# Attention values by seven block products, and a block's transfers issued from SP's queue

## The chip, the cores and the metric

The kernel runs on one core of one Trainium2 chip. The metric is the device time of one execution in microseconds (us). The median of three runs of the kernel before is 2158.83 us (2158.8 to 2162.86).

## The reference

The input `x` has 2048 rows of 256 numbers, in f32. It is normalized row by row, and two results are added to it:

```python
xn = layernorm(x)                                  # [2048, 256]
q, k, v = heads(xn @ Wqkv.T)                       # 16 heads, head size 128
w = softmax(q @ k.T / sqrt(128))                   # per head, [2048, 2048]
attn = concat(w @ v) @ Wout.T                      # Wout: [256, 2048]
ffn = bitlinear(sigmoid(bitlinear(xn, w1)) * bitlinear(xn, w2), w3)   # ternary weights, hidden 704
out = x + attn + ffn
```

## The kernel before

**Stages.** A lead-in of some 120 us normalizes `x`, keeps it transposed in SBUF (`xnT`, 128 partitions x 2 halves of the 256 features x 2048 rows), makes queries, keys and values of the first heads, and does the whole feed-forward part; its result goes to four DRAM tiles `yd0` to `yd3`, one for each 512 rows. Everything after that is attention.

**Blocks, quarters, groups.** A block is 512 query rows of one head: 16 heads x 4, 64 blocks. A block has four quarters of 128 rows. Two heads, that is 8 blocks, are a group, and 8 groups follow one another. One turn of the main loop is called a step here and named (block in its group, quarter): (1,3) is the last quarter of a group's second block. The order on every engine is the order in which the program's text issues, and every engine and queue works strictly in it.

**One step.** In step (b, t) TensorE does, in this order: the scores of a quarter six steps ahead (`scores`: 16 matmuls of 512 columns); a first side product; the weighted sum of this step's own quarter of the block (`weighted`, line 724: 32 matmuls of 256 columns, 16 in t = 3); a second side product, in most steps. VectorE does the reads that the step before left behind (`added`, lines 750 and 754, and the read of the second side product), two row maxima of the scores (line 579), their scale (582), the read of the first side product, in t = 2 the inverses of the softmax sums (624 to 627), and two transposes (line 657) of the quarter two steps back. ScalarE does the exponentials (589).

**The exchange.** The weights must be turned round. VectorE transposes only inside squares of 32 x 32, so each quarter's exponentials `p` are first moved between partitions into tiles `part`, by 12 DMAs of 64 KB. `exchanged` issues ten of them from SP's queue and two from ScalarE's (line 611). `part` has two buffers; an exchange thus needs that the transposes of two quarters back have been done.

**Products with fewer multiplications.** The weighted sum is done by a scheme of seven block products in place of eight; GpSimd makes the block differences for it (`differences`, line 677, in `R`; `v_combined`, line 699, in `st`). Queries and keys of the next head are made the same way (`fast_product`), four matmul instructions of 512 columns a product, from sums of `xnT` (`x_sums`, held in `ts`) and of the weights. So are the output projections of the group before (`o_product`, read by `o_read`, line 824). The values of the next group are made directly (`v_product`: 16 matmul instructions of 256 columns, two row tiles of both heads).

**Side products by place.** In quarters 2 and 3 of every block: queries and keys. In quarters 0 and 1 of blocks 0 to 3 of a group: output products of the group before. In quarters 0 and 1 of blocks 4 to 7: values of the next group. All side products use one PSUM buffer (`ps_m`, tag m), and the weighted sum another (`ps_av`); each is written anew only when its readers are done.

**What is moved about.** Attention results of a block go from `oU` to DRAM (`put_away`: `od`), and come back into three slots `o3` for the output products (`o_fetched`). The running sums of the output sit in `yd0` to `yd3`, and two at a time in SBUF (`osums`): `y_moved` loads or stores one of 512 KB. `inverses` stores the inverses of the softmax sums (`rd`) and `spread` loads them back spread over partitions (`oT`). `load_weights` loads 256 KB. All of these are issued from GpSimd's queue; their places are in the loop's body and in `between(n, t)`, which runs at the end of a step, after `exchanged`:

```python
if (a, t) == (0, 0):
    y_moved(b + 1, False)
...
elif (a, t) == (1, 0):
    o_fetched(g, b + 1, 1, 0)
...
elif (a, t) == (1, 3) and more:
    y_moved(b + 2, False)
```

Here `a` is the block's parity and `b` the even block, in blocks 0 to 3 of a group.

Of the kernel before, what the change touches and what calls it, by code (L numbers as in the profile page):

```python
# [20 lines left out]
def layernorm_attention_bitffn_kernel(  # L21
# [132 lines left out]

    def x_sums(c: int):
        t = apool.tile([P, 4, QB], F32, tag=f"t{c}", name=f"t{c}", bufs=1)
        x00, x10 = (xnT[:, d, bass.ts(c, QB)] for d in range(KC))
        x01, x11 = (xnT[:, d, bass.ts(c + 1, QB)] for d in range(KC))
        for i, (a, b) in enumerate(((x01, x00), (x11, t[:, 0]), (x11, x01), (x10, t[:, 1]))):
            nc.gpsimd.tensor_tensor(t[:, i], a, b, ALU.subtract)  # L160
        ts[c] = t

    def fast_product(h: int, b: int, i: int, second: bool):

        c = b // 2 * 2
        wk, wq = (weights[h // G, i][:, :, bass.ts(h % G, D)] for i in "kq")
        w, t = ws[h], ts[c]
        x00, x10 = (xnT[:, d, bass.ts(c, QB)] for d in range(KC))
        x11 = xnT[:, 1, bass.ts(c + 1, QB)]
        lhs, rhs = {  # L170
            (0, 0): ((wk[:, 0], x00), (w[:, 1], t[:, 1])),
            (0, 1): ((w[:, 2], t[:, 2]), (wq[:, 1], t[:, 3])),
            (1, 0): ((w[:, 0], t[:, 0]), (w[:, 3], x11)),
            (1, 1): ((wk[:, 1], x10),),
        }[b % 2, i][second]
        pm = ps_m.tile([P, QB], F32, tag="m", name=f"pw{h}_{b}_{i}_{int(second)}")
        in_halves(pm, lhs, rhs, True, True)
        return pm

    def fast_read(h: int, b: int, i: int, second: bool, pm):  # L180
        c = b // 2 * 2
        if (b % 2, i) == (0, 0):
# [9 lines left out]
            for j in (c, c + 1)  # L192
        )
        q0, q1 = qTs[h, c], qTs[h, c + 1]
# [66 lines left out]
    wxs = {}  # L261
# [10 lines left out]
    def v_product(g: int, m: int, second: bool):  # L272
        w = weights[g, "v"]
        pm = ps_m.tile([P, 2, G * D], F32, tag="m", name=f"pvw{g}_{m}")
        for j in range(2):
            for d in range(KC):
                in_halves(
                    pm[:, j], xnT[:, d, bass.ts(2 * m + j, P)], w[:, d], d == 0, d == KC - 1
                )
        return pm  # L280

    def v_read(g: int, m: int, second: bool, pm):
        for j in range(G):
            nc.vector.tensor_copy(
                v_tile(g * G + j)[:, 2 * m : 2 * m + 2], pm[:, :, bass.ts(j, D)]
            )

# [11 lines left out]
        for g in range(2)  # L299
    ]  # L300
# [314 lines left out]
    def inverses(n: int):  # L615
# [12 lines left out]
        nc.gpsimd.dma_start(rds[n % 2], riT)  # L628

    def spread(n: int):  # L630

        if n < NBK - NB:
            r = rds[n % 2].rearrange("(j c) r -> j (c r)", c=32)[:, : TB * 32]
            nc.gpsimd.dma_start(
# [152 lines left out]
    def o_fetched(g: int, b: int, head: int, slot: int):  # L787
        nc.gpsimd.dma_start(o3[:, slot], ods[g % 2][b][:, head])
# [4 lines left out]
    def y_moved(b: int, back: bool):  # L793
        y, yd = osums[:, 1 - b % 2], yds[b]
        nc.gpsimd.dma_start(*((yd, y) if back else (y, yd)))
# [133 lines left out]
    def between(n: int, t: int):  # L929
# [3 lines left out]

        if t == 1:
            if i == GB - 1 and n < last:
                load_weights(g, "o", nc.gpsimd)
        if t == 2:
            if i == NB - 1 and g + 1 < H // G:
                load_weights(g + 1, "v", nc.gpsimd)
            elif n == last - 1:  # L940
                load_weights(g, "o", nc.gpsimd)
        if g and i < NB:
            o_moved(g - 1, i, t)
        elif n < last:
# [6 lines left out]
            elif (i, t) == (GB - 1, 2):  # L951
                y_moved(0, False)
        if n < last and (i, t) == (GB - 1, 3):
            o_sums(g)
        if n >= last - 1 and t == 2:
            b = n + 1 - last
            nc.gpsimd.dma_start(o3[:, b % 2], ods[(H - 2) // G % 2][b][:, 0])
        if (n, t) in ((last - 2, 3), (last - 1, 0)):
# [5 lines left out]
    with tc.manual_schedule():  # L964
        for u in range(-LEAD, (NBK - 1) * TB):
# [13 lines left out]
            if n >= NB and t < 2:  # L979
# [5 lines left out]
                elif g + 1 < H // G:  # L985
                    seven, hi = True, (g + 1, j)
                    product, read, twice = v_product, v_read, False
# [153 lines left out]
```

## Time and profile before

| | |
|---|---|
| median of the runs | 2158.83 us |
| the profiled execution | 2159.7 us, its span 2157.9 us |
| TensorE (PE) busy | 2143.5 us, granted clock 1.0 |
| VectorE (DVE) busy | 1756.1 us |
| ScalarE (ACT) busy | 1375.1 us |
| GpSimd (POOL) busy | 1579.3 us |
| DMA | 304.34 MB, mean 141 GB/s |
| SP's hardware queue | 175.21 MB; GpSimd's software queue 91.97 MB |

Instructions of GpSimd that issue a DMA (DMA_DIRECT2D) count as busy. Those of SP don't; SP has no busy time in the page. In the lists of groups a row reads: line of the kernel, engine, operation, tile written and tiles read, shapes, number; busy time in all, mean ns of one; idle time of the engine ahead of it and what ended that. Mean durations of matmuls overlap, so the timeline's distances between starts say more. In a timeline a row reads: start, duration, engine, line, operation, tiles, number of merged instructions, and in brackets the idle time before it and what released it. Rows of transfers end with the median us from issue to landing.

### The profile page before, as it was taken

How to read it: one execution, taken by the hardware profiler on the slowest of the kernel's cores; microseconds unless marked ns; L12 is line 12 of the kernel's file. 1: busy time of each engine (PE TensorE's matmuls, PEld its weight loads, DVE VectorE, ACT ScalarE, POOL GpSimd, SP SyncE). 2: the span in 40 equal slices, each digit the busy share in tenths (PEclk: the TensorE clock that was granted, in tenths of full speed). 3: DMA queues.
4: the chain of work that ended last, by engine and by line, in shares of the span. 5: the costliest groups of instructions: out<-in, count | busy, mean ns of one | idle time of the engine just before them, and what ended most of it. 6: DMA issues, size and time to landing. Idle time of an engine off the chain costs nothing. (4 is left out here: it accounts for less than half of the span.)

```text
span 2157.9 us, 41390 instructions
## 1 busy us (share of the span) xinstructions
PE 2143.5 (99%) x14018; PEld 1207.6 (56%) x14018; DVE 1756.1 (81%) x2394; ACT 1375.1 (64%) x2414; POOL 1579.3 (73%) x1010
## 2 busy tenths in 40 slices
PE   9999999999999999999999999999999999999999
PEld 6745445445655555555555455655555555555556
DVE  6577887888888887888788888788888888788885
ACT  5587766666666666666666666666666666666773
POOL 0067767987678867887768876788767887788873
PEclk9999999999999999999999999999999999999999
DMA  2055555575556655566555754556555665556663
GB/s 94 39 119 139 132 117 136 148 187 142 121 140 160 166 141 128 136 184 157 123 128 142 189 151 110 140 145 180 149 122 135 157 173 143 127 138 184 174 151 95
DMA packets 182341, 304.34 MB, mean 141 GB/s; under 512 B 55088, under 2 KB 60592, under 8 KB 182128
## 3 DMA queue, kind: packets, MB, share of 16 engines
q1 hardware_dynamic: 127856, 175.21, 31.9%
q0 software_dynamic: 28720, 91.97, 17.5%
q10 hardware_dynamic: 25552, 34.51, 6.2%
q8 instruction: 111, 1.82, 0.4%
q14 instruction: 102, 0.84, 0.1%
HBM read 65.60 MB, written 34.54 MB: 46 GB/s over the span
## 5 line engine op out<-in xcount | busy, mean ns | idle before, releaser
L677 POOL TENSOR_TENSOR R<-R 128x1024 f32<-128x1024 f32 x441 | 1175.5, 2673 | 144.4 <-DVE R L657 84.7
L94 PE MATMUL s<-kT,qT 128*64 128x512 f32 x4000 | 907.4, 592 | 1.0 <-ACT p L589 0.8
L613 ACT COPY part<-p 32x512 f32<-32x512 f32 x1024 | 630.7, 616 | 417.7 <-issue 306.5
L579 DVE TENSOR_REDUCE mx<-s 128x1 f32<-128x1024 f32 x512 | 618.2, 1220 | 230.5 <-PE s L94 216.7
L589 ACT ACTIVATE p<-s,nm 128x1024 f32<-128x1024 f32 x512 | 565.9, 1110 | 207.8 <-PE pw L94 101.6
L657 DVE STREAM_TRANSPOSE R<-part 128x1024 f32<-128x1024 f32 x512 | 605.1, 1220 | 34.1 <-DMA part<-p 24.4
L94 PEld LDWEIGHTS s<-kT,qT 128*64 128x64 f32 x4000 | 331.7, 137 | 476.2 <-issue 431.8
L724 PE MATMUL av<-R,v 128*64 128x256 f32 x3728 | 531.2, 379 | 1.5 <-DVE oU L750 1.3
L724 PE MATMUL av<-R,st 128*64 128x256 f32 x3024 | 457.7, 379 | 2.5 <-ACT oU L742 1.3
L724 PEld LDWEIGHTS av<-R,v 128*64 128x64 f32 x3728 | 357.7, 137 | 109.7 <-issue 43.9
L724 PEld LDWEIGHTS av<-R,st 128*64 128x64 f32 x3024 | 305.5, 137 | 143.0 <-issue 50.6
L628 POOL DMA_DIRECT2D rd<-r x60 | 33.4, 556 | 154.2 <-DVE r L627 153.9
L742 ACT COPY oU<-av 64x256 f32<-64x256 f32 x248 | 90.7, 366 | 84.5 <-PE av L724 77.0
L780 POOL DMA_DIRECT2D od<-oU x60 | 34.0, 567 | 125.0 <-DVE oU L754 125.0
L750 DVE TENSOR_TENSOR oU<-av,oU 64x256 f32<-64x256 f32 x248 | 101.8, 411 | 27.4 <-ACT oU L742 24.7
L94 PE MATMUL pvw<-wv,xnT 128*64 128x256 f32 x896 | 107.6, 379 | 0.0
L94 PEld LDWEIGHTS pvw<-wv,xnT 128*64 128x64 f32 x896 | 74.8, 137 | 45.7 <-issue 24.2
L589 ACT ACTIVATION_READ_ACCUMULATOR p<-s,nm 128x1 f32 x512 | 100.3, 196 | 0.0
L824 DVE TENSOR_TENSOR osums<-pow,osums 128x512 f32<-128x512 f32 x108 | 72.5, 682 | 29.3 <-DMA osums<-yd 18.3
L94 PE MATMUL pw<-t,ws 128*64 128x512 f32 x336 | 88.4, 592 | 0.0
L160 POOL TENSOR_TENSOR t<-xnT 128x512 f32<-128x512 f32 x4 | 5.1, 1271 | 107.1 <-DMA part<-p 107.1
L200 DVE TENSOR_TENSOR kT<-pw,kT 128x512 f32<-128x512 f32 x112 | 76.8, 686 | 1.8
(153 smaller groups left out, 1484.4 us busy)
## 6 DMA issues: line engine op xcount, KB each, us to landing
part<-p SPq DMA_DIRECT2D x2560, 64.0 KB, 2.3
part<-p ACTq DMA_DIRECT2D x512, 64.0 KB, 2.6
o<-od POOLq DMA_DIRECT2D x74, 256.0 KB, 3.9
oT<-rd POOLq DMA_DIRECT2D x60, 256.0 KB, 5.5
od<-oU POOLq DMA_DIRECT2D x60, 256.0 KB, 2.7
osums<-yd POOLq DMA_DIRECT2D x28, 512.0 KB, 4.8
yd<-osums POOLq DMA_DIRECT2D x26, 512.0 KB, 3.5
yd<-yT SPq DMA_DIRECT2D x4, 512.0 KB, 2.6
```

The lines of the kernel that those rows point to most:

```text
L94: nc.tensor.matmul(out[c * HP : (c + 1) * HP], lhs[:, c * HP : (c + 1) * HP], rhs, start=start, stop=stop, skip_group_check=True,)
L200: nc.vector.tensor_tensor(k, pk, base, ALU.add)
L579: nc.vector.tensor_reduce(mx[:, i : i + 1], s, AX.X, ALU.max)
L589: nc.scalar.activation(p, s, AF.Exp, bias=nm, scale=SCALE, accum_out=sums[n][:, t, i : i + 1],)
L613: nc.scalar.copy(*ends(j, j))
L657: nc.vector.transpose(to[:, t % 2, 2 * i : 2 * i + 2], part.rearrange("p g (s c) -> p g s c", s=2),)
L677: nc.gpsimd.tensor_tensor(o, x, y, ALU.subtract)
L724: nc.tensor.matmul(av[i * HP : (i + 1) * HP, half], l[:, kk], moving(s, kk), start=start, stop=(k == units[r] - 1), skip_group_check=True,)
L742: nc.scalar.copy(u[op, oq], av[ap, half])
L750: nc.vector.tensor_tensor(u[p, q], av[p, half], u[p, q], ALU.add)
L780: nc.gpsimd.dma_start(ods[h // G % 2][b][:, h % G], oU)
L824: nc.vector.tensor_tensor(to, pm, y, ALU.add)
```

## The change

Values of groups 1 to 7 are made by seven block products per half of the rows, 14 a group, each four matmul instructions of 512 columns, with 16 reads of 128 x 512. The products come out transposed, so each head's half (512 KB) is stored to DRAM by four DMAs (`v_sent`), loaded back as one (`v_landed`) into a stretch of `xnT` that no product reads any more (`landing`), and transposed by VectorE into place (`v_transposed`). To free that stretch, the second pair of row blocks changes its order (`pair`). GpSimd makes the sums of the value weights (`v_sums`), and two of its combinations of values move from the start to the end of the last step of a group.

All the transfers named above but `put_away`'s, and but a few at the very end of the kernel, go from GpSimd's queue to SP's. Their places in the program's text stay.

```diff
+    def pair(c: int):
+        return (c, c + 1) if c == 0 else (c + 1, c)
...
+    def v_sums(g: int):
+        wv = weights[g, "v"]
+        sums_of(wv[:, :, D:], wv[:, :, :D], f"wvs{g}")
...
-    def v_product(g: int, m: int, second: bool):
...
+    def fast_v_product(g: int, m: int, second: bool):
+        half, m = divmod(m, NB)
+        wv, w, t = weights[g, "v"], wxs[f"wvs{g}"], ts[2 * half]
+        c0, c1 = pair(2 * half)
+        x00, x10 = (xnT[:, d, bass.ts(c0, QB)] for d in range(KC))
+        x11 = xnT[:, 1, bass.ts(c1, QB)]
+        lhs, rhs = (
+            ((wv[:, 0, D:], x00), (w[:, 1], t[:, 1])),
+            ((w[:, 2], t[:, 2]), (wv[:, 1, :D], t[:, 3])),
+            ((w[:, 0], t[:, 0]), (w[:, 3], x11)),
+            ((wv[:, 1, D:], x10),),
+        )[m][second]
+        pm = ps_m.tile([P, QB], F32, tag="m", name=f"pvw{g}_{half}_{m}_{int(second)}")
+        in_halves(pm, lhs, rhs, True, True)
         return pm
...
+    def fast_v_read(g: int, m: int, second: bool, pm):
...
+        if (m, second) == (0, False):
+            nc.vector.tensor_copy(k0, pm)
+            return
+        todo = {
+            (0, True): ((k1, k0),), (1, False): ((q1, k1),), (1, True): ((q0, q1),),
+            (2, False): ((q1, q1), (k1, k1)), (2, True): ((k1, k1),), (3, False): ((k0, k0),),
+        }[m, second]
+        for o, i in todo:
+            nc.vector.tensor_tensor(o, pm, i, ALU.add)
+
+    def v_sent(h: int, half: int):
+
+        v = v_half(h, half).rearrange("p k d -> p (k d)")
+        vd = vds[h % G][half].rearrange("(j r) (q c) -> q r j c", r=32, c=S // 8)
+        for q in range(P // 32):
+            nc.sync.dma_start(vd[q], v[bass.ts(q, 32)].rearrange("r (j c) -> r j c", c=S // 8))
+
+    def v_landed(h: int, half: int):
+        nc.sync.dma_start(landing, vds[h % G][half])
+
+    def v_transposed(h: int, half: int):
+        v = v_half(h, half).rearrange("p k (q r) -> p q k r", r=32)
+        w = landing.rearrange("p (q k r) -> p q k r", q=P // 32, r=32)
+        for u in range(2):
+            nc.vector.transpose(v[:, 2 * u : 2 * u + 2], w[:, 2 * u : 2 * u + 2])
+
+    wxs, landing = {}, xnT[:, 0, QB : 3 * QB]
...
-        nc.gpsimd.dma_start(rds[n % 2], riT)
+        nc.sync.dma_start(rds[n % 2], riT)
...
-            nc.gpsimd.dma_start(
+            nc.sync.dma_start(
                 oT.rearrange("p (j x) -> p j x", j=P // 32), r.partition_broadcast(P)
             )
...
-        nc.gpsimd.dma_start(o3[:, slot], ods[g % 2][b][:, head])
+        nc.sync.dma_start(o3[:, slot], ods[g % 2][b][:, head])
...
-        nc.gpsimd.dma_start(*((yd, y) if back else (y, yd)))
+        nc.sync.dma_start(*((yd, y) if back else (y, yd)))
...
+        v_steps = {
+            (5, 1): [(v_sent, 0, 0)],
+            (5, 3): [(v_transposed, 0, 0), (v_sent, 1, 0)],
+            (6, 1): [(v_landed, 1, 0)], (6, 3): [(v_transposed, 1, 0)],
+            (7, 1): [(v_sent, 0, 1)], (7, 3): [(v_transposed, 0, 1)],
+            (8, 1): [(v_sent, 1, 1)], (8, 3): [(v_landed, 1, 1)], (9, 1): [(v_transposed, 1, 1)],
+        }
         if t == 1:
             if i == GB - 1 and n < last:
-                load_weights(g, "o", nc.gpsimd)
+                load_weights(g, "o")
         if t == 2:
             if i == NB - 1 and g + 1 < H // G:
-                load_weights(g + 1, "v", nc.gpsimd)
+                load_weights(g + 1, "v")
             elif n == last - 1:
-                load_weights(g, "o", nc.gpsimd)
+                load_weights(g, "o")
...
+        for late in range(2):
+            if late < g + 1 < H // G + late:
+                for do, j, half in v_steps.get((i + late * GB, t), ()):
+                    do((g + 1 - late) * G + j, half)
+        if t == 3 and i == GB - 1 and g + 1 < H // G:
+            v_combined((g + 1) * G, 0)
+            v_combined((g + 1) * G, 1)
...
+        if t == 3:
+            if i == NB - 1 and g + 1 < H // G:
+                v_sums(g + 1)
...
-                    product, read, twice = v_product, v_read, False
+                    product, read, twice = fast_v_product, fast_v_read, j % NB != NB - 1
...
                 if n % 2 and n % GB < NB <= n < NBK - NB - 2:
                     y_moved(n % GB, True)
+                if n >= 0 and n % GB in (5, 7) and n // GB + 1 < H // G:
+                    v_landed((n // GB + 1) * G, n % GB // 2 - 2)
                 differences(n + 1, "T3a")
-                if n >= 0 and blocks[n + 1][1] == 0:
+                if n >= 0 and (n + 1) % GB == NB:
                     v_combined(blocks[n + 1][0], 0)
                     v_combined(blocks[n + 1][0], 1)
...
-                    load_weights(h // G + 1, "qk"[v % TB], nc.gpsimd)
+                    load_weights(h // G + 1, "qk"[v % TB])
```

More of the change, by code (lines that the diff above doesn't have):

```diff
@@ L153, in weight_sums @@
         ws[h] = w
+    def pair(c: int):
+        return (c, c + 1) if c == 0 else (c + 1, c)
     def x_sums(c: int):
         t = apool.tile([P, 4, QB], F32, tag=f"t{c}", name=f"t{c}", bufs=1)
-        x00, x10 = (xnT[:, d, bass.ts(c, QB)] for d in range(KC))
-        x01, x11 = (xnT[:, d, bass.ts(c + 1, QB)] for d in range(KC))
+        c0, c1 = pair(c)
+        x00, x10 = (xnT[:, d, bass.ts(c0, QB)] for d in range(KC))
+        x01, x11 = (xnT[:, d, bass.ts(c1, QB)] for d in range(KC))
         for i, (a, b) in enumerate(((x01, x00), (x11, t[:, 0]), (x11, x01), (x10, t[:, 1]))):
@@ L167, in fast_product @@
         w, t = ws[h], ts[c]
-        x00, x10 = (xnT[:, d, bass.ts(c, QB)] for d in range(KC))
-        x11 = xnT[:, 1, bass.ts(c + 1, QB)]
+        c0, c1 = pair(c)
+        x00, x10 = (xnT[:, d, bass.ts(c0, QB)] for d in range(KC))
+        x11 = xnT[:, 1, bass.ts(c1, QB)]
         lhs, rhs = {
@@ L191, in fast_read @@
             kTs[h].rearrange("p (j k r) -> p k j r", j=P // 32, r=32)[:, j * TB : (j + 1) * TB]
-            for j in (c, c + 1)
+            for j in pair(c)
         )
-        q0, q1 = qTs[h, c], qTs[h, c + 1]
+        q0, q1 = (qTs[h, j] for j in pair(c))
         pk = pm.rearrange("p (k j r) -> p k j r", j=P // 32, r=32)
@@ L255, in v_place @@
         return (k + NKT // 2) % NKT if h == 1 else k
-    wxs = {}
+    def v_sums(g: int):
+        wv = weights[g, "v"]
+        sums_of(wv[:, :, D:], wv[:, :, :D], f"wvs{g}")
     def sums_of(k, q, name: str):
@@ L270, in sums_of @@
         wxs[name] = w
-    def v_product(g: int, m: int, second: bool):
[L273 to L279, printed above, removed]
-        return pm
[L282 to L285, printed above, removed]
-            )
+    def fast_v_product(g: int, m: int, second: bool):
+        half, m = divmod(m, NB)
+        wv, w, t = weights[g, "v"], wxs[f"wvs{g}"], ts[2 * half]
+        c0, c1 = pair(2 * half)
+        x00, x10 = (xnT[:, d, bass.ts(c0, QB)] for d in range(KC))
+        x11 = xnT[:, 1, bass.ts(c1, QB)]
+        lhs, rhs = (
[6 more added lines that the diff above has]
+        in_halves(pm, lhs, rhs, True, True)
+        return pm
@@ new lines, in v_half @@
+    def v_half(h: int, half: int):
+        return v_tile(h)[:, half * NKT // 2 : (half + 1) * NKT // 2]
+    def fast_v_read(g: int, m: int, second: bool, pm):
+        half, m = divmod(m, NB)
+        q, k = (
+            v_half(g * G + i, half).rearrange("p k d -> p (k d)").rearrange(
+                "p (j k r) -> p k j r", j=P // 32, r=32
+            )
+            for i in range(G)
+        )
+        k0, k1, q0, q1 = (
+            i[:, j % 2 * TB : (j % 2 + 1) * TB] for i in (k, q) for j in pair(2 * half)
+        )
+        pm = pm.rearrange("p (k j r) -> p k j r", j=P // 32, r=32)
+        if (m, second) == (0, False):
[7 more added lines that the diff above has]
+            nc.vector.tensor_tensor(o, pm, i, ALU.add)
@@ L299, in layernorm_attention_bitffn_kernel @@
         for g in range(2)
+    ]
+    vds = [
+        [away.tile([P, S // 2], F32, tag=f"vd{h}{i}", name=f"vd{h}{i}") for i in range(2)]
+        for h in range(G)
     ]
```

## The prediction

> **What bounds the kernel now.** I read the page first: busy times, costliest groups, transfers. This is its part 1 and one group.
>
> ```profile
> PE 2143.5 (99%) x14018; PEld 1207.6 (56%) x14018; DVE 1756.1 (81%) x2394; ACT 1375.1 (64%) x2414; POOL 1579.3 (73%) x1010
> ...
> L94 PE MATMUL pvw<-wv,xnT 128*64 128x256 f32 x896 | 107.6, 379 | 0.0
> ```
>
> TensorE is the bound: work taken from it is gained, and whatever makes it wait is lost. GpSimd has room; relieving it is worth nothing by itself. The timeline of TensorE gives real prices, as distances between starts (times of one group's blocks; all groups look alike):
>
> ```profile
> 1158.03 1.06 PE L94 MATMUL pow<-o,wo 128*64 128x512 f32 x4
> 1158.88 1.46 PE L724 MATMUL av<-R,v 128*64 128x256 f32 x11
> ...
> 1202.80 1.03 PE L94 MATMUL pow<-o,wos 128*64 128x512 f32 x4
> ...
> 1221.71 1.03 PE L94 MATMUL pow<-o,wo 128*64 128x512 f32 x4
> ...
> 1226.75 1.08 PE L94 MATMUL pow<-o,wos 128*64 128x512 f32 x4 [0.56 <-DVE osums L824]
> ...
> 1286.12 1.93 PE L94 MATMUL pvw<-wv,xnT 128*64 128x256 f32 x16
> 1287.85 3.65 PE L724 MATMUL av<-R,v 128*64 128x256 f32 x32
> ```
>
> A value product of the old form takes 1.73 us (1286.12 to 1287.85); a block product of 4 matmuls of 512 columns takes 0.86 (1158.03 to 1158.88). The bracket at 1226.75 is one of the few waits: the second product of a step shares its one accumulator with the first, so it waits until VectorE has read that; and that read waited for a transfer. The change moves that transfer, so I looked at when the exchange occupies SP, in windows of one step each (line 611; first and last start):
>
> ```profile
> L611 SPq DMA_DIRECT2D part<-p x10: 507/590/1082, 1083.6 to 1089.9; - x10
> ...
> L611 SPq DMA_DIRECT2D part<-p x10: 507/588/760, 1148.1 to 1154.0; - x10
> ...
> L611 SPq DMA_DIRECT2D part<-p x10: 534/591/1545, 1162.2 to 1169.2; - x10
> ...
> L611 SPq DMA_DIRECT2D part<-p x10: 507/555/604, 1194.0 to 1200.5; - x10
> ...
> L611 SPq DMA_DIRECT2D part<-p x10: 507/546/762, 1219.2 to 1226.6; - x10
> ```
>
> These belong to steps (5,2), (7,2), (0,0), (1,0), (1,3), named as block in its group and quarter. Ten issues hold SP for 6.5 to 7.5 us, and they can't start before VectorE's transposes of that step have freed the tiles. TensorE starts the next step at 1084.02, 1148.58, 1163.20, 1195.05 and 1218.28: SP works off a step's exchange during the next step. GpSimd, by contrast, issues at the end of the step itself, and the readers come soon after (timelines of GpSimd and VectorE):
>
> ```profile
> 1164.24 0.55 POOL L795 DMA_DIRECT2D osums<-yd  x1
> ...
> 1195.12 0.56 POOL L788 DMA_DIRECT2D o<-od  x1
> ...
> 1218.96 0.55 POOL L795 DMA_DIRECT2D osums<-yd  x1
> ```
> ```profile
> 1169.76 1.29 DVE L824 TENSOR_TENSOR osums<-pow,osums 128x512 f32<-128x512 f32 x2 [1.42 <-DMA osums<-yd]
> ...
> 1225.91 0.69 DVE L824 TENSOR_TENSOR osums<-pow,osums 128x512 f32<-128x512 f32 x1 [1.84 <-DMA osums<-yd]
> ```
>
> Those readers already wait for transfers issued some 6 us before them. Last, the page's transfers (median us to landing):
>
> ```profile
> part<-p SPq DMA_DIRECT2D x2560, 64.0 KB, 2.3
> ...
> o<-od POOLq DMA_DIRECT2D x74, 256.0 KB, 3.9
> ...
> osums<-yd POOLq DMA_DIRECT2D x28, 512.0 KB, 4.8
> yd<-osums POOLq DMA_DIRECT2D x26, 512.0 KB, 3.5
> yd<-yT SPq DMA_DIRECT2D x4, 512.0 KB, 2.6
> ```
>
> **TensorE's gain.** In each of 7 groups 8 old products, 13.84 us, give way to 14 block products, 12.04: 1.80 us, 12.6 in all. A change of 0.2%, 4.3 us, is about what can be told from none.
>
> **What costs nothing, and its cover.** Per group VectorE gets 16 reads of 0.68 (line 824's row) for 16 copies of 0.42, and 8 transposes of half a line-657 form, 0.6 each: 10 us, in a half group where it is busy 105 of 129 us. The reads follow the pattern of the output products, which TensorE bears; the transposes of (6,3), and of (1,1) in the next group, have two steps' notice. GpSimd gets four weight differences (2.2 us, as its output ones) and loses some 270 DMA issues of 0.55 to 0.78, about 170 us. The stores of the sums, the stores and broadcasts of the inverses and the q and k weights are wanted a step or more after they land. If that cover fails for the inverses, line 754's multiply waits, and TensorE's accumulator after it.
>
> **What the queue costs.** A landing from SP is taken as GpSimd's row less what the two 512 KB store rows differ by, 3.5 - 2.6 = 0.9: 3.9 us for 512 KB, 3.0 for 256 KB. Ends: 2.6 (SP's store) and 4.8 (GpSimd's load) for the first, 2.3 (a 64 KB part) and 3.9 for the second; single landings differ more, but seven groups add up. No site can gain more than the waits that it has, and TensorE's idle time is 14.4 us in all, so I leave the low ends at nothing or above. Per group, TensorE's new waits, with ends in brackets:
>
> 1. The sums of blocks 2 and 3, loaded at the ends of (1,3) and (2,0). The first load now stands behind the exchange whose issues end at about 1227.0; it lands at 1230.9, its add (0.7) ends at 1231.6, and the product of 1226.75 starts then: 4.9 late. The transposes of (2,0) stand behind that add on VectorE; their first half frees SP at 1232.8, ten issues take 6.5, and the load of block 3 starts at about 1239.5 and lands at 1243.5; two adds end at 1244.8. TensorE, with scores of (2,1) from 1232.5 and a step of 7.75, wants the accumulator at 1243.7: 1.1 late. VectorE then has transposes 2.4, two line-750 adds 0.8, maxima 2.4, scale 0.2, read 0.7: 1251.3, while TensorE's second product is due after 0.86 + 3.43, at 1249.1: 2.2 late. Together 8.2 (5.6 to 10.0).
> 2. Block 1's sums, end of (0,0): issued at 1169.8, landed at 1173.7, two adds done at 1175.0. (0,1) has no second product; the next scores, from 1170.94, take 3.43, so the accumulator is wanted at 1174.4: 0.6. The same 6.5 us on VectorE against 4.3 on TensorE: 2.2. Together 2.8 (1.5 to 3.7).
> 3. An output slot, loaded at the ends of (1,0) and (3,0) for the second product of the next step: issued at 1201.1, landed at 1204.1, wanted at 1202.80: 1.3 twice, 2.6 (1.2 to 4.4).
> 4. The value weights, end of (3,2): the exchange ends at 1283.2, they land at 1286.2 and are wanted at 1286.12: 0.1 (0 to 1.0).
> 5. The new return of the values at (5,3). It stands ahead of that step's exchange, but behind that of (5,2), which ends at 1090.6; the four new stores and the inverses' store ahead of that one use up SP's wait there (2.3 us). Issued at 1091.0, landed at 1094.9; two transposes (1.2) and line 750 (0.4) end at 1096.5. TensorE, with scores of (6,0) from 1090.04 and a product, wants the attention accumulator at 1090.04 + 3.43 + 0.86 = 1094.33: 2.2 late, and 0.3 for the read behind it: 2.5 (1.2 to 3.4).
> 6. The same at (7,3), behind more issues, one of them a 512 KB load that shares the engines: issued at 1156.0, landed at about 1160.5, line 750 done at 1162.1, wanted at 1158.88: 3.2, and 0.6 for the read before the second product: 3.8 (2.5 to 6.0, the last if the two loads follow one another). GpSimd's two combinations wait there too, until 1161.7 and not 1154.1; with them 2.6, its four weight differences 2.2, a store 0.6 and two block differences 4.8 end at 1171.9, where TensorE, 3.8 late, wants them at 1167.5 + 3.8: 0.6, left to the high end.
>
> Sum 20.0 us a group (12.0 to 28.5), 140 in seven (84 to 199). Against the profiled execution, 2159.7 us (span 2157.9): 2159.7 - 12.6 + 140 = 2287.1. The median of the runs, 2158.83, is 0.9 lower, so 2286; ends 2230 and 2346.
>
> The Trainium skill speaks differently in two places; nothing above rests on them. SP's rows show ten issues ahead of each load. "DMA: Bandwidth & Descriptors" (Issuing engines are not separate DMA queues) says that starting transfers from several engines saves only the sequencer's issue time, usually small beside the transfer; by it, gathering them on SP costs issue time alone, and with SP's idle time as cover the sum would be 2146. The same page (Anatomy of one DMA, SWDGE path) fits 2.0 us plus the bytes at 436 GB/s; an estimate by that page is 3.2 us for 512 KB, where GpSimd's row has 4.8, and with it, between my low and middle sums, the time would be about 2256.
>
> **Rivals.** *The loads arrive in time*: 2159.7 - 12.6 - 0.9 = 2146. For it: TensorE's gain is certain in count, and VectorE and SP have idle time on average. Against: block 2's sums would have to be issued before 1222, while SP is at the exchange from 1219.2 to 1226.6 and is in order. It decides if new waits stay under 1.8 us a group. Chance 0.07.
>
> *SP itself runs out.* Its 2560 exchange issues at their usual distance, 0.634 us, take 1623 us, and its list of waits holds 393 at line 611: together the 2024 us from the first issue to the last. 413 added issues (273 moved, 140 new) are 262 us. The waits can take them all or, if they are due to VectorE's pace, none; at half, 2159 - 13 + 131 = 2277. For it: block 1 then has 51 issues, 32.3 us, in 31.8. Against: most of the waits are for VectorE and leave room block by block. Chance 0.10; the time is in the same range.
>
> *VectorE alone*: loads are early enough, but a third of its 10 us a group reaches TensorE: + 23 - 12.6, 2169. Chance 0.05. Against: the output half has nearly the same load and 0.6 us of waits in 128.
>
> *The waits cancel the gain*, within 0.2%: it takes 1.2 to 2.4 us a group, under my low sum; 0.03.
>
> That the products don't shrink isn't a rival: the order of instructions has 14 a group.
>
> **How the numbers follow.** My forecast has 0.75, and with SP's and VectorE's rivals slower has 0.90; no change 0.03; faster 0.07. The range reaches below my low sum, for waits that overlap, and stops short of the high ends all together: 2195 to 2350 leaves out the faster and equal cases, the VectorE one and a small rest above.
>
> **What would show it.** Right: PE's busy time falls by about 12, its idle time grows by some 20 us a group; waits of line-824 adds on osums' loads of 4 to 7 us, of the new transposes on xnT's landing of 3 to 4, and SP's loads starting just after the tenth exchange issue. Wrong at step 1 if the adds wait under 2 us; wrong at 5 and 6 if the transposes don't wait; wrong altogether if TensorE's idle time stays under 25 us. If it grows with no wait on a landing, it was SP's pace or VectorE.

## The result, and the profile after

The changed kernel takes 2509.33 us (median of five runs, 2503.59 to 2515.97) against 2161.01 in five runs of the kernel before beside it: a ratio of 1.1613 [1.1589, 1.1637]. The profiled execution took 2515.97 us, its span 2514.2. The sign was forecast; the size was not: 348 us lost in place of 127, far above the range.

The page of the changed kernel, part 1 and the row of TensorE's clock in part 2:

```profile
PE 2232.1 (89%) x13514; PEld 1127.6 (45%) x13514; DVE 1821.1 (72%) x2450; ACT 1375.5 (55%) x2414; POOL 1423.5 (57%) x765
...
PEclk9999999999998999989998899989999999999899
```

TensorE has 504 matmul instructions fewer and is busy 89 us longer. Its idle time, span less busy time, is 282.1 us where it was 14.4. Both can be put into one sum against the profiled executions: -12.6 (the work removed), +267.7 of idle time, and 101.2 of busy time over the 2130.9 that were due (2143.5 - 12.6): 356.3, which is 2515.97 - 2159.7.

The costliest groups that wait (busy us, mean ns; idle time before them and what ended most of it):

```profile
L780 PE MATMUL av<-R,v 128*64 128x256 f32 x3728 | 561.2, 398 | 114.1 <-DVE oU L806 114.0
L880 DVE TENSOR_TENSOR osums<-pow,osums 128x512 f32<-128x512 f32 x108 | 72.4, 681 | 191.4 <-DMA osums<-yd 113.1
L94 PE MATMUL pow<-o,wos 128*64 128x512 f32 x224 | 74.8, 750 | 114.4 <-DMA o<-od 69.4
L335 DVE STREAM_TRANSPOSE v<-xnT 128x512 f32<-128x512 f32 x56 | 36.1, 683 | 128.4 <-DMA part<-p 70.3
```

Lines have moved: 724 is now 780 (weighted sum), 824 is 880 (adds of the sums), 750 is 806, 611 is 667 (exchange), 657 is 713, 795 is 851; 326, 329 and 335 are the values' stores, returns and transposes. The first and third rows are TensorE, 228.5 us of idle time in two groups of rows: weighted sums that wait for VectorE's read of the accumulator, and second output products that wait for a slot or for the sums. The second and fourth are VectorE, which waits at the same places for what SP brings.

TensorE's timeline at three of these places, (6,0), (1,1) and (2,0) (in brackets the idle time):

```profile
1240.63 3.63 PE L94 MATMUL s<-kT,qT 128*64 128x512 f32 x16
1244.06 1.06 PE L94 MATMUL pvw<-xnT,wv 128*64 128x512 f32 x4
1251.63 5.58 PE L780 MATMUL av<-R,v 128*64 128x256 f32 x32 [6.51 <-DVE oU L806]
...
1387.27 1.98 PE L94 MATMUL pow<-o,wos 128*64 128x512 f32 x4 [6.37 <-DMA o<-od]
...
1420.27 1.98 PE L94 MATMUL pow<-o,wos 128*64 128x512 f32 x4 [6.29 <-DVE osums L880]
```

The waits stand where the prediction put them, but they are long, and what follows them is slow: 5.58 us for 32 matmuls that took 3.65 before, 1.98 for four that took 1.03. The table by stretches around (6,0) shows why (length; busy time and instructions of PE, PEld, DVE, ACT and POOL; then the granted clock, DMA share and GB/s):

```profile
1240.60:1245.10 4.50, 4.50 (x23) 1.55 (x18) 2.03 (x2) 3.00 (x7) 0.00 (x0) 1.00 0.44 103
1245.10:1251.60 6.50, 0.02 (x1) 0.00 (x0) 1.73 (x3) 1.35 (x3) 0.00 (x0) 0.78 0.58 161
1251.60:1255.00 3.40, 3.37 (x16) 1.95 (x18) 3.32 (x5) 0.00 (x0) 2.37 (x2) 0.50 0.67 180
1255.00:1262.00 7.00, 7.00 (x42) 2.91 (x40) 5.48 (x7) 5.13 (x9) 6.92 (x4) 0.96 0.50 128
```

The clock falls to half 3.6 us after TensorE went idle and stays there 6.83 us, well into the work. The trace has 267 us at half clock; before it had 2.4.

And this is why the waits are long: the issues of SP's queue, in the timeline, around the returns of the values at (6,0) and (0,0) and before the sums' load of (1,3) (start, time from first to last issue, number):

```profile
1231.51 1.22 SPq L667 DMA_DIRECT2D part<-p  x2
1232.78 2.05 SPq L326 DMA_DIRECT2D vd<-v  x4
1234.92 0.40 SPq L684 DMA_DIRECT2D rd<-r  x1
1235.43 9.86 SPq L667 DMA_DIRECT2D part<-p  x10
1245.39 0.53 SPq L329 DMA_DIRECT2D xnT<-vd  x1
...
1303.00 11.29 SPq L667 DMA_DIRECT2D part<-p  x10
1314.40 0.52 SPq L83 DMA_DIRECT2D wo<-in_woutT_dram  x1
1314.96 1.98 SPq L326 DMA_DIRECT2D vd<-v  x4
1317.04 0.38 SPq L684 DMA_DIRECT2D rd<-r  x1
1317.53 6.56 SPq L667 DMA_DIRECT2D part<-p  x10
1324.13 0.58 SPq L851 DMA_DIRECT2D osums<-yd  x1
1324.75 0.45 SPq L329 DMA_DIRECT2D xnT<-vd  x1
...
1407.31 8.34 SPq L667 DMA_DIRECT2D part<-p  x10
1415.70 0.58 SPq L851 DMA_DIRECT2D osums<-yd  x1
```

Each load stands right behind the tenth issue of an exchange, as forecast. But that exchange is late itself. The one of (5,2) starts behind the four stores and takes 9.86 us, not 6.5, since two of its issues wait until an earlier part has landed: the return leaves at 1245.39, 4.8 us after the scores of (6,0) began, where the prediction had 0.96. At (0,0) it leaves at 1324.75, 8.6 us after the scores of 1316.12, where the prediction had 1.4. In the median over the groups, SP's exchange of (7,3) ends 15.6 us after the next scores start; before it was 7.4.

The landings, in contrast, are nearly as taken (KB, median us): the prediction had 3.9 and 3.0 for 512 and 256 KB. The returns of (0,0) alone took 5.5, and the prediction had 4.5 there.

```profile
o<-od SPq DMA_DIRECT2D x70, 256.0 KB, 3.1
...
vd<-v SPq DMA_DIRECT2D x112, 128.0 KB, 3.0
xnT<-vd SPq DMA_DIRECT2D x28, 512.0 KB, 4.4
osums<-yd SPq DMA_DIRECT2D x28, 512.0 KB, 3.7
```

### The profile page after: what moved, and what is told of

It is laid out like the page before. It is cut to its first block, busy times and chain, and to the rows that moved or that the text cites. A ratio compares the mean times of both kernels' runs of the same rounds, so it can differ in the third digit from the quotient of the medians.

```text
span 2514.2 us, 40546 instructions
## 1 busy us (share of the span) xinstructions
PE 2232.1 (89%) x13514; PEld 1127.6 (45%) x13514; DVE 1821.1 (72%) x2450; ACT 1375.5 (55%) x2414; POOL 1423.5 (57%) x765
## 5 line engine op out<-in xcount | busy, mean ns | idle before, releaser
L94 PE MATMUL s<-kT,qT 128*64 128x512 f32 x4000 | 944.0, 609 | 1.0 <-ACT p L645 1.0
L780 PE MATMUL av<-R,v 128*64 128x256 f32 x3728 | 561.2, 398 | 114.1 <-DVE oU L806 114.0
L780 PEld LDWEIGHTS av<-R,st 128*64 128x64 f32 x3024 | 295.8, 137 | 170.5 <-issue 62.4
L94 PE MATMUL pow<-o,wos 128*64 128x512 f32 x224 | 74.8, 750 | 114.4 <-DMA o<-od 69.4
L335 DVE STREAM_TRANSPOSE v<-xnT 128x512 f32<-128x512 f32 x56 | 36.1, 683 | 128.4 <-DMA part<-p 70.3
L847 POOL TENSOR_TENSOR o<-o 128x512 f32<-128x512 f32 x56 | 71.5, 1277 | 95.7 <-DMA o<-od 90.0
L94 PEld LDWEIGHTS pow<-o,wos 128*64 128x64 f32 x224 | 16.6, 158 | 140.3 <-issue 96.1
L755 POOL TENSOR_TENSOR st<-v 128x512 f32<-128x512 f32 x15 | 19.1, 1276 | 104.9 <-DVE v L335 104.9
```

The costliest lines, as they stand in the source:

```text
L94: nc.tensor.matmul(out[c * HP : (c + 1) * HP], lhs[:, c * HP : (c + 1) * HP], rhs, start=start, stop=stop, skip_group_check=True,)
L335: nc.vector.transpose(v[:, 2 * u : 2 * u + 2], w[:, 2 * u : 2 * u + 2])
L780: nc.tensor.matmul(av[i * HP : (i + 1) * HP, half], l[:, kk], moving(s, kk), start=start, stop=(k == units[r] - 1), skip_group_check=True,)
L847: nc.gpsimd.tensor_tensor(o3[:, slot], o3[:, x], o3[:, y], ALU.subtract)
```

## The experiments

Theory: two things were missing from a sum that had the right places. SP falls behind by several us, not by one exchange; and the half clock doubles the time of the work after each long wait. Rivals: the value part itself is what costs; it is the order in SP's queue alone; it is the traffic of the bigger transfers.

**The two halves of the change.** The value part alone, with all transfers but the exchange's on GpSimd's queue:

```diff
-            nc.sync.dma_start(vd[q], ...)      # and every other one of the change
+            nc.gpsimd.dma_start(vd[q], ...)
```

> The value part alone: every transfer that the change moved, and the new stores and returns of the values too, issue from GpSimd's queue. Queue theory (the new time comes from loads that stand on SP behind an exchange): TensorE's saving is left, 12.6 us, and GpSimd has 140 more issues of 0.56 (11 us a group) that it has room for: 2147 to 2160, the granted clock back at 1.0. Product theory (the new reads, transposes and the wait for the values' return cost the time by themselves): the stalls in front of (6,0) and (0,0), about 22 of the 50 us a group, stay: 2300 or more.

2182.85 us, 1.0107 [1.0092, 1.0122]. From its page:

```profile
PE 2143.3 (98%) x13514; PEld 1060.5 (49%) x13514; DVE 1820.5 (84%) x2450; ACT 1374.9 (63%) x2414; POOL 1671.8 (77%) x1178
```

The clock is full but for the last 3.5 us. The gain is there: steps (5,1) and (7,1) take 7.75 us and not 8.6, together the 1.8 forecast. It is more than eaten around the change of group, where steps are longer than before: (7,0) by 0.9 us, (0,0) 1.0, (0,1) 0.6, (0,2) 1.1, (0,3) 1.1, (1,0) 0.2. A loss of 23 us that the prediction had as a gain of 12.6. Busy time has not fallen by 12.6 either, at full clock. A matmul of 256 columns is recorded for 379 ns though the next one starts some 0.11 us later, so each wait leaves about 0.27 us (an estimate from these two) in the busy time, and only the rest shows as idle: 36.5 us, 22 more than before.

The kernel before with its transfers moved to SP:

```diff
-        nc.gpsimd.dma_start(o3[:, slot], ods[g % 2][b][:, head])   # and rds, oT, osums, weights
+        nc.sync.dma_start(o3[:, slot], ods[g % 2][b][:, head])
```

> The queue part alone: values as before, all the moved transfers on SP. Order theory (each load pays for the exchange ahead of it): the stalls at the output loads stay, those of (1,1), (2,0) and (3,1), about 28 us a group, those of the values' return go: 2159 + 7 x 28 = 2355. Load theory (SP has more issues than time): 273 of 413 added issues are left, so about two thirds of 350 + 13: 2400; or little, if SP's idle time takes them all: under 2200. Product theory: 2159.

2346.09 us, 1.0858 [1.0842, 1.0874], 107.9 us at half clock. The queue is the greater part: 186 of the 348 us without any new product. The stalls are those of the output half alone: in groups 1 to 7 a mean idle time of 7.1 us at (2,0), 3.0 at (1,1), 3.8 at (3,1), 2.3 at (0,2). The value part alone loses 23 us; the other 139 come with the values' stores and returns on SP's queue.

**The clock by itself.** The kernel before, with four, then eight, idle reductions on VectorE in (5,3) of seven groups, so that nothing but a wait is added:

```diff
+                if t == 3 and n % GB == 5 and n < NBK - GB:
+                    for _ in range(4):                                  # stall8: 8
+                        nc.vector.tensor_reduce(sink, xnT[:, 0, :HALF], AX.X, ALU.max)
```

> The cost of a stall by itself: the kernel before, with four idle reductions of 128 x 1024 (about 1.2 us each, result unused) on VectorE at the end of (5,3) of the first seven groups. VectorE has 2.7 us before TensorE wants the accumulator in (6,0), so TensorE idles about 2.2 us seven times. Both theories: 15 us more, no low clock, since the changed kernel's stalls under 2.3 us showed none.

2176.59 us, 1.0082 [1.0067, 1.0097]. TensorE waits 2.03 us in each group, 14.2 in all; after three of the seven waits the clock is half for 3.41 us, where none was expected. Its busy time grows by 5.0.

> The same with eight reductions: TensorE idles about 7.1 us seven times. Idle theory (a stall costs its idle time): 50 us more than before, granted clock 1.0. Clock theory (after a stall of more than about 2.5 us the granted clock falls to a half for some 7 us): 50 + 7 x 3 = 71 us more, PE's busy time up by about 20, mean clock about 0.99.

2223.77 us, 1.0304 [1.0287, 1.0321], 64.6 us longer than the kernel before beside it (2159.16). The idle time is 7 x 7.04 = 49.3; TensorE's busy time grows by 16.2, from 2143.5 to 2159.7, with the same work: 65.5 in all. Idle time alone, without a clock, falls short. One of the seven stalls by stretches:

```profile
1386.00:1389.50 3.50, 3.50 (x26) 1.48 (x22) 3.43 (x4) 2.08 (x5) 0.00 (x0) 1.00 0.56 134
1389.50:1394.50 5.00, 0.02 (x2) 0.00 (x0) 4.86 (x5) 0.45 (x1) 0.00 (x0) 1.00 0.28 66
1394.50:1401.40 6.90, 4.84 (x24) 2.76 (x26) 6.73 (x10) 1.45 (x3) 3.77 (x3) 0.51 0.11 40
1401.40:1405.00 3.60, 3.60 (x26) 1.49 (x24) 2.48 (x4) 2.07 (x5) 3.58 (x3) 1.00 0.35 94
```

The wait comes first, at full clock; the half clock follows. No SP transfer was moved here, so the half clock comes from waiting as such, and here each wait costs a third more than its length (16.2 / 49.3). The work agrees: TensorE is busy for 32.8 us at half clock, and half of that is 16.4.

**Order or pace of SP.** In the changed kernel, the transfers of a step's end are issued before its exchange:

```diff
+            ahead = u >= 0 and more and n < NBK - NB
+            if ahead:
+                if t == 0:
+                    differences(n, "T2l")
+                between(n, t)
...
-            if u >= 0:
+            if u >= 0 and not ahead:
```

> The changed kernel, with the transfers that stand at the end of a step issued ahead of that step's exchange and not behind it; the same number of issues on SP. Order theory: each load goes out 6 to 7 us earlier, nearly all of the waits of 5 to 11 us shrink to 0 to 4, and with them the time at low clock: 2150 to 2250. Load theory: SP has as much to do as before and is as late: 2450 to 2510.

2405.57 us, 1.1128 [1.111, 1.1147]. The waits at (0,2) and (1,1) go, and nearly that at (3,1) (0.1 us); (2,0) grows to 9.6 us of idle time, (6,0) and (0,0) keep 7.3 and 8.8. The median lag of SP's exchange grows through the output blocks to 20 us. Order is worth 104 us and lies between the two theories; it does not heal SP's pace.

Two of the ten exchange issues go to ScalarE:

```diff
-    SP_DMAS = 10
+    SP_DMAS = 8
```

> The changed kernel, with 8 of the 12 exchange transfers on SP and 4 on ScalarE's queue, not 10 and 2: SP is relieved of 1.27 us a step, 5 us a block, about as much as it was given; the order is the same. Load theory: SP's lag of 4 to 7 us in the blocks from (5,2) on goes, and the stalls fall to what my prediction had, 20 us a group, plus the low clock that follows the longer ones: 2280 to 2340. Pure order theory: loads still stand behind an exchange of 5.1 us, 1.3 shorter: about 2450. ScalarE gets 1.06 us a step more and might itself be late, which would show as waits on its exponentials.

2397.1 us, 1.1098 [1.1072, 1.1125], between the two expected. 512 issues fewer on SP, some 300 us of its time, bring 112. So SP is not simply full: it waits more instead, 811 us in place of 625 between its records. That each issue counts where it stands ahead of something awaited fits this, but the run doesn't show it by itself.

**Place by place.** Three single cuts in the changed kernel, and one addition to the value part:

```diff
-            (5, 3): [(v_transposed, 0, 0), (v_sent, 1, 0)],
+            (5, 3): [(v_sent, 1, 0)], (6, 0): [(v_transposed, 0, 0)],      # late_turn
...
-            nc.sync.dma_start(vd[q], ...)
+            nc.gpsimd.dma_start(vd[q], ...)                                # sent_pool
...
-        nc.sync.dma_start(o3[:, slot], ods[g % 2][b][:, head])
+        nc.gpsimd.dma_start(o3[:, slot], ods[g % 2][b][:, head])           # o_pool, and y_moved's
...
-        nc.gpsimd.dma_start(landing, vds[h % G][half])
+        nc.sync.dma_start(landing, vds[h % G][half])                       # return_sp
```

> The changed kernel, with VectorE's transposes of the returned values moved from the end of (5,3) to the end of (6,0), one step later; the queues are as in the change. Order theory: the stall of 9 us in (6,0) goes and the others stay: 2509 - 7 x 9 = 2446. Load theory (SP's pace is the bound, a stall only lets it catch up): SP goes on late and the stall comes back further on, at (0,0) above all, where 11 us become 14 to 18; 2470 to 2510.

2461.58 us, 1.1407 [1.1388, 1.1426]: the wait at (6,0) goes, 48 us with it, and (7,0) waits 2.7 in place of 0.7. The lag of SP's exchange at (7,3) is still 14.2 us: it is not caused by this stall.

> The changed kernel, with the 112 stores of the values (v_sent) back on GpSimd's queue and all else on SP. Load theory: SP loses 16 issues of 0.6 us a group, 10 us, in the stretch where its lag grows, so the stalls of (6,0), (0,0) and (1,1) shrink by some 10 us idle a group and their low clock: 2509 - 7 x 13 = 2420. Order theory: the loads still stand behind an exchange, and only the 2 us of stores ahead of the returns are gone: 2509 - 7 x 4 = 2480.

2439.13 us, 1.1307 [1.1274, 1.134]. The 112 stores of the values, for which nothing on TensorE waits directly, cost 70 us by standing in SP's queue: 0.63 us each. That is the distance of two issues there, but no fixed price: the 512 issues of the run above brought 0.22 each.

> The changed kernel, with the loads and stores of the output's sums and slots (y_moved, o_fetched) back on GpSimd's queue: 18 fewer issues a group on SP. Order theory: the stalls of (0,2), (1,1), (2,0) and (3,1) go, 28 us a group, those of (6,0) and (0,0) stay: 2509 - 196 = 2313. Load theory: SP's lag in blocks 5 to 7 is smaller as well, so (6,0) and (0,0) shrink too: 2250 to 2300.

2380.94 us, 1.1035 [1.1019, 1.105], above both ranges: with the sums and the attention results back on GpSimd, sites 2 and 3 vanish, site 1 shrinks to 1.7 us of idle time, and 128 us go with them. (0,0) keeps 9.5 us a group and (6,0) 5.5, and (4,0), the value weights, now waits 4.0.

> The value part with only the 28 returns (v_landed) on SP; everything else issues from GpSimd, the values' stores too. This is steps 5 and 6 of the prediction by themselves, with SP hardly loaded more than before. If the prediction's sizes were right but for SP's lag, TensorE idles about 2.2 us in (6,0) and 3.2 in (0,0), and the time is that of the value part alone, 2183, and 7 x 5.5 and a little low clock: 2215 to 2230. If a return behind one exchange costs 6 and 11 us by itself, without a lag: 2183 + 7 x 20 = 2320.

2247.24 us, 1.0416 [1.0385, 1.0447], above the first range and far under the second case. The returns alone on SP add 64 us to the value part. TensorE waits 4.7 us a group at (6,0) and 2.6 at (0,0); the prediction had 2.2 and 3.2, and 2.5 and 3.8 with the reads behind. Here SP has nothing else added. The return leaves 0.5 us (median) after the scores of (6,0), earlier than forecast, but takes 6.3 us to land and not 3.9; why is open. At (0,0) the wait is below the forecast: the further 8 us there in the changed kernel come with the other issues in the queue.

**Issue time or bytes.** The changed kernel with the same moved transfers, but most of their bytes left out:

```diff
-        nc.sync.dma_start(landing, vds[h % G][half])
+        nc.sync.dma_start(landing[:, :32], vds[h % G][half][:, :32])
...
+        y, yd = y[:, :, :32], yd[:, :, :32]      # vd and o3 in the same way
```

> The changed kernel with the same moved transfers in the same order, but the stores and loads of the values, the loads of the attention results and the loads and stores of the running sums move 32 columns each only, 1/4 to 1/32 of their bytes; the rest of those data is left out of the computation. Theory A, SP is late by the number of its issues: the exchange of (7,3) still ends 13 us or more after the next scores start (15.6 in the changed kernel), and only the landings get shorter, by 1 to 1.5 us at some six sites a group: some 55 us of idle time and 25 of clock less, 2410 to 2450 us. Theory B, SP is late because it waits for big transfers to land (every eighth transfer before must be in): the lag falls to 6 to 9 us and the time to under 2350.

2344.56 us, 1.0853 [1.0835, 1.087]. From the page, the landings that are left:

```profile
vd<-v SPq DMA_DIRECT2D x112, 16.0 KB, 1.8
o<-od SPq DMA_DIRECT2D x70, 16.0 KB, 1.8
...
osums<-yd SPq DMA_DIRECT2D x28, 32.0 KB, 2.2
...
xnT<-vd SPq DMA_DIRECT2D x28, 16.0 KB, 1.9
```

Neither theory alone: the time is below what pure issue time was to give, and the lag at (7,3) is 12.4 us, far from the 6 to 9 of pure waiting. Adding up SP's records from the first exchange issue to the last gives the shares. Before, 2024 us are 1564 of issues and 460 of waits and short gaps. In the changed kernel 2380 are 1756 and 625. With few bytes 2210 are 1761 and 449. So with few bytes SP's stretch grows by 186 us with 197 us of added issues: the waits and gaps take up 11 of them. This is a sum and not a cause; in the run with fewer exchange issues the waits grew by 186. The other 165 go with the bytes: landings that come later, the half clock after longer waits (267 us of it against 118), and the exchange's own issues, held until other transfers have landed. These rows are from SP's lists of waits (total, times, longest), first before, then in the changed kernel:

```profile
SPq L611 <- DVE R L657: 206.1, 169, 3.2
SPq L611 <- DMA part<-p: 93.5, 107, 2.6
```
```profile
SPq L667 <- DVE R L713: 204.8, 75, 6.1
SPq L667 <- DMA part<-p: 156.1, 94, 7.0
SPq L667 <- DMA xnT<-vd: 18.1, 21, 2.5
```

The exchange's waits for VectorE have not grown; those for landings have, and one of them is for `xnT<-vd`, which the exchange doesn't read. How the 165 divide stays open.

**The value part off SP.** Five versions of the value part alone, towards one that keeps its gain:

```diff
-            (5, 3): [(v_transposed, 0, 0), (v_sent, 1, 0)],
-            (6, 1): [(v_landed, 1, 0)], (6, 3): [(v_transposed, 1, 0)],
-            (7, 1): [(v_sent, 0, 1)], (7, 3): [(v_transposed, 0, 1)],
+            (5, 3): [(v_sent, 1, 0)], (6, 0): [(v_transposed, 0, 0)],            # best_a; stores on SP
+            (6, 1): [(v_landed, 1, 0)], (7, 1): [(v_sent, 0, 1), (v_transposed, 1, 0)],
+            (7, 3): [(v_transposed, 0, 1)],
...
-        if n < last and (i, t) == (GB - 1, 3):
+        if n < last and (i, t) == (GB - 1, 2):                                   # best_b: + o_sums earlier
...
-            nc.sync.dma_start(vd[q], ...)
+            nc.gpsimd.dma_start(vd[q], ...)        # best_c: + stores on GpSimd; best_d: on nc.scalar
```

> A version that might beat both: the value part, the old transfers on GpSimd, the values' stores on SP, the returns on GpSimd, and the two transposes that stood in the short steps (5,3) and (6,3) moved to (6,0) and (7,1). Queue theory: the waits of (7,0) and of (0,1) to (0,3) in the value part alone, 4 us a group, go for the most part; 2150 to 2165 against 2159.

2236.6 us, 1.0364 [1.0347, 1.0382], far above the 2150 to 2165 expected. The stores of (7,1), behind SP's exchanges, came so late that the return, on GpSimd, waited for them: 3.5 us idle a group at (0,0).

> The same, with the output weights' four differences on GpSimd moved from the end of (7,3) to the end of (7,2), where GpSimd waits: they then no longer stand between the late combinations of values and the block differences that TensorE wants in (0,1). If GpSimd's order was what held (0,0) to (0,3): 2147 to 2158. If VectorE's load holds them: the same as the version without this move.

2224.27 us, 1.0298 [1.0278, 1.0318]: 12 us less, since the steps (0,1) to (0,3) are together 1.5 us a group shorter. The wait at (0,0) is as long; the weights' sums of the output, moved out of its way, were not what it waited for.

> The value part of the change alone, all moved transfers back on GpSimd's queue, the value stores and returns too; the transposes of (5,3) and (6,3) one step later, and the block sums' store and loads in (7,3) one quarter earlier. If only SP's queue and the early transposes cost, TensorE keeps its 1.8 us a group: 2147 to 2160. If GpSimd's late combinations around (0,0) to (1,0) keep their waits (3.9 us a group with the value part on GpSimd as written), 2165 to 2185.

2166.81 us, 1.0034 [1.0022, 1.0047], in the second range. (What this version moves to an earlier quarter is, as in the one before, the output weights' sums; the block sums' load and store are where the change has them.) The 112 stores off SP bring 57 us, and of the value part's losses those at (7,0), (0,1) and (0,2) are gone. Left are 1.1 us at (0,3), 0.2 at (1,0), and (0,0):

```profile
1160.47 3.67 PE L780 MATMUL av<-R,v 128*64 128x256 f32 x32 [1.37 <-DVE oU L806]
1165.23 1.08 PE L94 MATMUL pow<-o,wos 128*64 128x512 f32 x4 [1.09 <-DVE osums L880]
```

> As the kernel with everything on GpSimd, but the value stores issue from ScalarE's queue (16 a group, some 0.6 us each beside its exponentials, 1375 of 2160 us busy). If GpSimd's issue time was what made its combinations late, the waits at (0,x) shrink: 2147 to 2165. If ScalarE's exponentials then come late instead, 2165 to 2190.

2165.8 us, 1.0033 [1.002, 1.0045], no different: GpSimd's issues of the stores are not the rest.

> As the one before, and the returns of the values on ScalarE's queue too. If a queue with room is all that is missing, 2147 to 2160, at or under the kernel before; if the returns wait in ScalarE's queue for their stores and hold its exponentials back, 2170 to 2200.

The returns on ScalarE too: 2174.46 us, 1.0059 [1.0045, 1.0072], worse.

Last, the return of (7,3) ahead of that step's block difference, and the first sums' load behind it:

```diff
+                if n >= 0 and n % GB in (5, 7) and n // GB + 1 < H // G:
+                    v_landed((n // GB + 1) * G, n % GB // 2 - 2)
                 differences(n + 1, "T1a")
...
-            elif (i, t) == (GB - 1, 2):
+            elif (i, t) == (GB - 1, 3):
                 y_moved(0, False)
```

> The kernel with the value part alone on GpSimd and later transposes, with the return of the values issued ahead of the first block difference of (7,3), 2.3 us earlier, and the first sums' load one step later, behind it. If the remaining loss (7 us slower than before) is the landing of this one return at (0,0), 1.4 + 1.1 us idle on TensorE a group, and GpSimd's combinations that wait 4.7 us for it, then 2145 to 2155 and faster than before. If GpSimd is simply full around (0,0) to (1,0), 2160 to 2170.

2161.44 us (11 runs; before, over all its runs beside these, 2159.09), 1.0012 [1.0003, 1.0021]: within 0.2% of the kernel before, in the second of the ranges expected, that of a GpSimd which stays late. But the two moves together did count, 5 us against the version they start from; they were not separated. TensorE at (0,0):

```profile
1156.57 3.62 PE L780 MATMUL av<-R,v 128*64 128x256 f32 x32
1160.72 1.08 PE L94 MATMUL pow<-o,wos 128*64 128x512 f32 x4 [0.53 <-DVE osums L880]
```

The 1.37 is gone and 1.09 has become 0.53; in the mean of the groups 1.35 us of idle time at (0,0) have become 0.53. In each group 1.8 us are gained and 2.0 lost, by the length of the steps: 0.7 at (0,0), 1.1 at (0,3), 0.2 at (1,0). At (0,3) VectorE's transposes have waited 2.23 us for GpSimd's block difference; GpSimd is late since its combinations waited 2.46 us for the values:

```profile
1147.15 0.56 POOL L329 DMA_DIRECT2D xnT<-vd  x1
1147.73 4.82 POOL L733 TENSOR_TENSOR R<-R 128x1024 f32<-128x1024 f32 x2
1152.50 0.56 POOL L851 DMA_DIRECT2D osums<-yd  x1
1155.52 1.27 POOL L755 TENSOR_TENSOR st<-v 128x512 f32<-128x512 f32 x1 [2.46 <-DVE v L335]
```

> The same with the value stores on ScalarE's queue, which takes 2.2 us of issues off GpSimd in (7,1) and in (0,1). 2145 to 2152 if both the early return and room on GpSimd count; as the run beside it, within 3 us, if only the return does.

2162.53 us, 1.0017 [1.0008, 1.0025]: within 3 us of the one beside it, so GpSimd's time for these stores doesn't count. No version here beats the kernel before.

## Why the prediction was wrong, point by point

**TensorE's gain: right.** Steps (5,1) and (7,1) are 0.9 us shorter each in every kernel with the value part where no wait covers them. Busy time did not fall by 12: half clock adds to it in the changed kernel, and at full clock each new wait leaves a part of itself there.

**The places: right.** Idle time appeared at (0,0), (0,2), (1,1), (2,0), (3,1), (4,0) and (6,0), and hardly anywhere else (0.9 at (7,0), 0.7 at (7,1), 0.3 at (0,3)). Each load started behind the tenth exchange issue. The landing term was about right: medians of 3.7 and 4.4 for 512 KB and 3.1 for 256, with the returns of (0,0) 1 us over their forecast.

**The step that failed first: SP's time of issue.** The terms set each load's issue at the end of an exchange taken from the trace of before, with at most 1 us of lag. Measured mean idle times a group, with the forecast behind: (0,0) 10.6 (3.8), (1,1) 6.4 (1.3), (2,0) 7.3 (4.9, and 3.3 in the two steps after, which did not come), (3,1) 3.5 (1.3), (6,0) 6.3 (2.5), (0,2) 1.0 (2.8), (4,0) 0.8 (0.1). At the four largest sites the lag accounts for the difference. Against the start of the step's scores, the awaited load leaves later than forecast by 6.9 us at (0,0) (8.3 in place of 1.4), 5.1 at (1,1), 2.2 at (2,0) and 3.7 at (6,0), in the median; the waits there are longer by 6.8, 5.1, 2.4 and 3.8. The forecast counted the issues in front of one load; it did not carry the lag from step to step. SP's mean room over the whole kernel says little here: a group's issues stand in a few steps, and a late exchange makes the next late. At (1,1) the slot's load went out 11.2 us after the scores of that step, and 6.1 had been taken. Idle time is 128 of the 229 us over the forecast, and most of it is this. The rival on SP had this mechanism, but as a separate case at half of 262 us; it acts together with the waits for loads. Its own doubt, whether SP's waits take up the added issues, is answered for this kernel: in sum they took up none, and grew from 460 to 625 us.

**The step that was missing: the half clock.** The sum priced a wait at its length. The other 101 us of the excess are busy time. In the changed kernel TensorE is busy for 162.9 us at half clock, so some 81 of them come from the clock; of the other 20's kind the value part alone has 12, at full clock. At stall8's rate of a third (stall4 has the same, 5.0 on 14.2) the forecast's own 140 us of waits would have brought 47 us more: 2333, still in the range. At twice the rate they would have left it. SP's lag broke the range, and the longer waits then lost the clock too.

**What was costed at nothing: not quite nothing.** The value part alone loses 23 us. The transposes of (6,3) did not wait for their landing, as "two steps' notice" had it, but TensorE waited at (7,0) for a read that stood behind them on VectorE; 0.9 us a group went when they stood one step later. Around the change of group, where the prediction had 0.6 us for GpSimd's late combinations and left it to the high end, the steps are 4 us a group longer, and 2.0 in the best arrangement.

**Issue time beside the transfer.** Moving the old transfers alone to SP's queue took the kernel from 2160 to 2346 us; SP's records there hold 137 us more of issues than before. "DMA: Bandwidth & Descriptors" (Issuing engines are not separate DMA queues) of the Trainium skill says that several issuing engines save only the sequencer's time, usually small beside the transfer. In sum the issue time is the greater part here, but not all of the 186 us: an awaited load also stands behind the waits of the queue that it joins. "Usually small" does not hold for a queue that already has ten issues of 0.59 us in steps of 6 to 9 us.

**The signs of the prediction.** The adds wait for the sums' loads (8.47 us ahead of the product of 1420.27), the new transposes for their landing or for what stands before it (7.2 us at (6,0), forecast 3 to 4). Idle time grew by 38 us a group and not 20: the sign was right, its size was not.

## What to carry to other kernels

When transfers are gathered on a queue that is already busy, don't price each load behind one block of issues from the old trace: carry the queue's lag forward step by step, and count every issue, of stores that nobody waits for too, at up to its full distance (0.63 us here) as soon as something awaited stands behind it. A wait of the bounding engine has a second price, the clock that it loses; find from the trace when it is lost, and count it on top. And test the two halves of a change separately first: here the half that looked like a sure gain was a small loss by itself, and came near even only when one return was issued some 3 us earlier and one load a step later.

## What the runs showed of the hardware

The length of a wait alone does not decide whether the clock is lost; its place on a fixed grid does. Within each of these traces all stretches at half clock start on one grid of 3.413 us (to 0.004), and last 3.41 us or a multiple of it (to 13.65), but for one at the very end. Cut along this grid, the 20 traces have 12547 windows from 130 us on. Of those at full clock, all 254 in which TensorE was idle for more than 2.017 us were followed by half clock, and none of the 11818 with less than 1.92; between the two, 2 of 10 were. Of those at half clock, all 209 with more than 0.74 us of idle time were followed by another one, and all 256 with less than 0.73 by full clock.

So the half clock can begin when TensorE is working again, and the same wait can cost or not. In stall4 the seven waits are 2.03 us each: the three that lie whole in one window lost the clock, the four that are split between two did not. A wait of 3.65 us in the run with 8 exchange issues on SP, split as well, kept it; no wait over 4 us did.

"TensorE: Matmul & The Clock Gate" (Part 1: The HAM clock gate) of the Trainium skill has a free-running window of 3413 ns, which the grid agrees with; its rule of thumb, no idle gaps over some 3.4 us, is too generous for these traces, where 1.92 us was enough once and 2.03 always if it fell into one window.
